# Four graph layers on 32 graphs: the last graph's softmax sums taken by TensorE, layer 2's weights planned later, new entry delays for graphs 1 to 4

## The chip, the core and the metric

The kernel runs on one NeuronCore of one Trainium2 chip. A core has TensorE (PE in the profile; its weight loads are PEld), VectorE (DVE), ScalarE (ACT), GpSimd (POOL) and SyncE (SP), each with its own instruction queue, and 16 DMA engines that all queues share. The metric is the device time of one execution in microseconds (us), as the median of several runs; lower is better.

## The reference, cut to what matters

The input is 32 graphs of 512 nodes with 256 features, `x` of shape (32, 512, 256) in float32, and one adjacency matrix `adj` (512, 512) that all graphs share. Each graph goes through four layers, and each layer is an attention over the graph followed by a residual and a normalisation:

```
x = layernorm(x + L0(x, adj))   # 8 heads, softmax(q k^T / sqrt(32)), then a feed-forward pair w1, w2
x = layernorm(x + L1(x, adj))   # 1 head, e = leaky_relu(s1[i] + s2[j]), softmax, times h = x W
x = layernorm(x + L2(x, adj))   # e = leaky_relu((x W1)(x W2)^T), softmax, times x W3, relu
x = layernorm(x + L3(x, adj))   # 4 heads, e = leaky_relu(e_src[i] + e_dst[j]), softmax, elu
```

In every softmax the entries without an edge are masked out. The kernel computes the unnormalised weights p = exp(e) * edge, multiplies them with the values, and divides by the row sums of p afterwards. How those row sums are formed in layers 0 and 3 is what the change touches.

## The kernel before

**One graph, one chain.** Everything of a graph stays on the chip: a (512, 256) tile is loaded, goes through the four layers, and is stored. Nodes lie in NC = 4 chunks of 128 partitions, features in KC = 2 halves. Matmuls are in float32.

**An order written by a planner.** `fast_path` doesn't issue instructions as it goes. `plan(engine, ns, run, reads, writes, ...)` records an operation with an assumed duration, and `Plan.place` then walks a model of the five engines and of the DMA: again and again it takes the operation that can start earliest, and among those of one engine the one with the earliest due time (`urgency`), and issues it. So the source fixes a static order for each engine's queue. On the chip each engine takes its queue in that order and waits on semaphores. Due times come from graph number times `PACE` plus a curve `TENTHS` over the graph's own ranks; `START` gives the model's earliest time for the first operation of graphs 0 to 4; at most `WAYS` = 5 graphs are open at once. A slot (`p`: 8 buffers of 1 MB, `t`: 9, `bank`: the 8 PSUM banks, and others) is given out only if the graphs ahead can still be completed, which `safe` reads from a profile of how many slots a graph holds at each rank.

**Preparation.** `prepare` (graph -1 in the planner) loads and transforms the weights: `load` issues a DMA from SP and tells the planner with `lag` how long after the issue the data is there. Edge transposes are line 767, the folding of b1 is line 784, the transposes of layer 2's W1 and W2 line 831, and their product line 842. In `urgency`, preparation comes before any graph on every engine but SP.

**Row sums in layer 0.** For each half g and each chunk m, `exps` makes four score products (line 996) and four exponentials (line 1000), DVE multiplies with the edges (line 1018), and PE adds value products into a bank (line 1025). The row sums run beside that: `add_dma` (line 934) has GpSimd issue a DMA that adds one `p` buffer to another, (1 into 0), (3 into 2), (2 into 0); the two totals are then multiplied with a column of ones, `pick`, in line 1042: eight products, four of them in four different 32-column strips at a time. `rinv0` and `heads_out` (lines 947, 956, 979, 982) follow.

**Row sums in layer 3.** A `p` holds two chunks of two heads. DVE makes it in four scalings (line 1238) and one multiplication (line 1245), PE uses it in line 1254. After the second `p` of a half, two DMAs add it to the first and then fold the halves of the result; line 1269 multiplies the totals with `pick`. Lines 947, 964, 979 and 982 divide, lines 1277 to 1282 finish the elu, lines 907 to 917 normalise, and line 1296 stores.

Of the kernel before, what the change touches and what calls it, by code (L numbers as in the profile page):

```python
# [25 lines left out]

WAYS = 5
PACE = 90.76
START = (0, 0, 60.35, 91.65, 156.14)
LAST = ()  # L30
STAY = 3.96
TENTHS = (0, 30.43, 93, 94.94, 170.51, 206.64, 280.32, 312.71, 390.11, 381.83, 480.02)
@with_exitstack
def general_path(
    ctx: ExitStack,
# [408 lines left out]
class Plan:  # L444
# [62 lines left out]
    def place(self, urgency, ways, stay=0.0, run=True):  # L507


        held_by = {g: self.profile(g) for g in {self.ops[0].graph, self.ops[-1].graph}}  # L510
        engines = {e: 0.0 for e in (PE, DVE, ACT, POOL, SP, DMA)}
        waiting = {e: [] for e in engines}
        free = {k: [(0.0, i) for i in range(n)] for k, n in self.counts.items()}
# [9 lines left out]
        def safe(op, kind, new):  # L523
            spare = len(free[kind]) - len(new)
            if spare < 0:
                return False
            have = spare
            for g in order:
                mine = held.get((g, kind), [])
                have += len(mine)  # L530
                if g == op.graph:
                    have += len(new)
                    mine = mine + new
                r, rows = front[g], held_by.get(g, held_by[self.ops[-1].graph])[kind]
                ahead = sorted(s.first for s in mine if s.first > r)
                for i, stop in enumerate(ahead + [len(rows)]):
                    if stop > r and max(rows[r:stop]) + len(ahead) - i > have:
                        return False
                    r = max(r, stop)
                if g == op.graph:  # L540
                    return True
# [70 lines left out]
def fast_path(  # L612
# [87 lines left out]
    def T(slot):  # L700
        return slot.tile if slot.kind is None else buffers[slot.kind][slot.index]
# [23 lines left out]
    odd = keep("odd", [P, NC])  # L725

    def prepare():
        def load(dst, to, src, lag=3000):
            def run():
                with nc.allow_non_contiguous_dma(reason="columns, once"):  # L730
                    nc.sync.dma_start(to(T(dst[0] if isinstance(dst, tuple) else dst)), src)
            plan(SP, 450, run, [], [dst], lag=lag)
# [268 lines left out]
                T(p)[:, j, :], T(banks[j]), AF.Exp, scale=1.0 / math.sqrt(D0)),  # L1001
                [banks[j]], [(p, j)])

    def layer0(xs):
        xT = transposed(xs)
        qT, kT, v = Slot("t"), Slot("t"), Slot("v")
        for k in range(KC):
            project_t(wqkv, C + k * P, xT, kT, k)
            project_t(wqkv, k * P, xT, qT, k)
        project(xT, wqkv, 2 * C, C, v)  # L1010

        oT, sm, totals = Slot("t"), Slot("bank"), []
        for g in range(KC):
            av, ps = Slot("bank"), []
            for m in range(NC):
                p = Slot("p")
                exps(kT, qT, g, m, p)
                dve(2420, lambda p=p, m=m: nc.vector.tensor_tensor(  # L1018
                    T(p), T(p), T(edge_t)[:, m, :].unsqueeze(1).to_broadcast([P, J, N]), ALU.mult),
                    [p, (edge_t, m)], [p], True)  # L1020

                def run(p=p, m=m, g=g, av=av):
                    for j in range(J):
                        h = g * J + j
                        nc.tensor.matmul(T(av)[j * D0:(j + 1) * D0, :],  # L1025
                                         T(v)[:, m, h * D0:(h + 1) * D0],
                                         T(p)[:, j, :], start=(m == 0), stop=(m == NC - 1))
                plan(PE, 880, run, [(v, m), p], [av], tiling=2)
                ps.append(p)
                if m % 2:  # L1030
                    add_dma(ps[m - 1], p)
                if m == 3:
                    add_dma(ps[0], ps[2])
                total = ps[0]

            totals.append(total)
            evac(oT, lambda t, g=g: t[:, g, :], av, lambda b: b, N, [(oT, g)])

        def run():
            for g, p in enumerate(totals):  # L1040
                for j in range(J):
                    nc.tensor.matmul(T(sm)[j * 32:(j + 1) * 32, :], pick[:, g, :], T(p)[:, j, :],  # L1042
                                     start=(g == 0), stop=(g == KC - 1))
        plan(PE, 1740, run, totals, [sm], tiling=2)
        rinv = rinv0(sm)
        t = heads_out(oT, rinv, H0)

        def check():
            r = T(rinv)[:, :NC * H0]
            nc.vector.scalar_tensor_tensor(fit, r, R_MIN, fit, ALU.is_gt, ALU.min)  # L1050
            nc.vector.scalar_tensor_tensor(fit, r, R_MAX, fit, ALU.is_lt, ALU.min)
        dve(370, check, [rinv], [], True)
        for c0 in range(0, NC, 2):
            add(t, t, xs, c0)
        n1 = Slot("y")
        normalise(t, n1)
        for c0 in range(0, NC, 2):
            add(xs, xs, None, c0, be2_row)
        nT = transposed(n1)
        y = Slot("y")  # L1060
        for c0 in range(0, NC, 2):
            add(y, n1, None, c0, g1_row, ALU.mult)
            add(y, y, None, c0, bb_row)
        hT = Slot("t")
        for d in range(KC):
            bank = Slot("bank")

            def run(bank=bank, d=d):
                for k in range(KC):
                    nc.tensor.matmul(T(bank), T(w1_sb)[:, k, d * P:(d + 1) * P], T(nT)[:, k, :],  # L1070
                                     start=(k == 0), stop=(k == KC - 1))
            plan(PE, 1720, run, [w1_sb, nT], [bank])
            act(690, lambda bank=bank, d=d: nc.scalar.activation(
                T(hT)[:, d, :], T(bank), AF.Relu, bias=T(b1_sb)[:, d:d + 1]), [bank, b1_sb], [(hT, d)])
        f = Slot("y")
        for c0 in range(0, NC, 2):
            bank = Slot("bank")

            def run(bank=bank, c0=c0):
                for j in range(2):  # L1080
                    for k in range(KC):
                        nc.tensor.matmul(T(bank)[:, j * C:(j + 1) * C],  # L1082
                                         T(hT)[:, k, (c0 + j) * P:(c0 + j + 1) * P],
                                         T(w2_sb)[:, k, :], start=(k == 0), stop=(k == KC - 1))
            plan(PE, 1730, run, [w2_sb, hT], [bank])
            dve(680, lambda bank=bank, c0=c0: nc.vector.tensor_tensor(
                T(f)[:, c0:c0 + 2, :], T(bank).rearrange("p (c d) -> p c d", c=2),
                T(y)[:, c0:c0 + 2, :], ALU.add),
                [bank, (y, c0), (y, c0 + 1)], [(f, c0), (f, c0 + 1)])
        normalise(f, f)  # L1090
        for c0 in range(0, NC, 2):
            w, parts = slice(c0, c0 + 2), (c0, c0 + 1)
            dve(690, lambda w=w: nc.vector.tensor_tensor(
                T(f)[:, w, :], T(f)[:, w, :], T(g2_row).unsqueeze(1).to_broadcast([P, 2, C]),
                ALU.mult), [(f, c) for c in parts] + [g2_row], [(f, c) for c in parts], True)
            dve(690, lambda w=w: nc.vector.tensor_tensor(
                T(f)[:, w, :], T(f)[:, w, :], T(xs)[:, w, :], ALU.add),
                [(s, c) for s in (f, xs) for c in parts], [(f, c) for c in parts], True)
        return f
# [122 lines left out]
            add(y, y, xs, c0)  # L1222
        return y

    def layer3(xs):
        xT = transposed(xs)
        totals = []
        q, G, oT, sm = Slot("v"), Slot("p"), Slot("t"), Slot("bank")
        project(xT, l3w, 0, C + 2 * H3, q)
        e1, e02 = gates(q, H3, G)  # L1230
        for k in range(KC):
            av = Slot("bank")
            for m0 in range(0, NC, 2):
# [22 lines left out]
                                             T(p)[:, 2 * m + i, :], start=(m0 + m == 0),  # L1256
                                             stop=(m0 + m == NC - 1))
                plan(PE, 1770, run, [q, p], [av], tiling=3)
                if m0 == 0:
                    total = p  # L1260
                else:
                    add_dma(total, p)
                    add_dma(total, None)

            totals.append(total)
            evac(oT, lambda t, k=k: t[:, k, :], av, lambda b: b, N, [(oT, k)])
        def run():
            for h in range(H3):
                nc.tensor.matmul(T(sm)[32 * h:32 * h + 32, :], pick[:, 0, :],  # L1269
                                 T(totals[h // 2])[:, h % 2, :], start=True, stop=True)  # L1270
        plan(PE, 870, run, totals, [sm], tiling=2)
        t = heads_out(oT, rinv3(sm), H3)

        e, y = Slot("y"), Slot("y")
# [10 lines left out]
        return y  # L1285

    def graph(b):
        xs = Slot("x")
        plan(SP, 450, lambda xs=xs: nc.sync.dma_start(
            T(xs), x[b].rearrange("(c p) d -> p c d", p=P)), [], [(xs, c) for c in range(NC)],  # L1290
            lag=9000)
        for layer in (layer0, layer1, layer2, layer3):
            y = layer(xs)
            xs = Slot("x")
            normalise(y, xs)
        plan(SP, 450, lambda: nc.sync.dma_start(
# [80 lines left out]
```

## Time and profile before

| | before |
|---|---|
| median of 3 runs | 3004.08 us (3002.78 to 3010.93) |
| profiled span | 3009.1 us, mean granted TensorE clock 0.985 |
| PE busy | 2903.1 us (96%) |
| DVE, ACT, POOL busy | 2361.4 us (78%), 1963.8 us (65%), 951.3 us (32%) |
| accumulating DMAs of 1 MB, line 934 | 256, 7.6 us median from issue to landing |
| accumulating DMAs of 0.5 MB, line 934 | 64, 5.3 us median |

The page is read from the top: which engine is busy, then in which slices of the span it isn't, then the chain of work that ended last. An engine that is busy in nearly the whole span bounds the kernel in its middle; what is left are the two ends, where the chain of waits names what the engine stood still for.

### The profile page before, as it was taken

The page shows a single profiled execution, that of the slowest core. Times are in us where ns is not written, and L with a number is a line of the kernel's source. Part 1 is how long each engine was busy: PE and PEld are TensorE (multiplying, and loading weights), DVE is VectorE, ACT ScalarE, POOL GpSimd, SP SyncE. Part 2 cuts the span into 40 slices and gives each one's busy share as a digit, 9 for nine tenths or more (in the row PEclk, how much of TensorE's full clock was granted, in tenths as well). Part 3 has the DMA queues.
Part 4 walks back from the last instruction along what each step waited for, and adds up shares of the span by engine and source line. Part 5 has one row for each costly group of instructions (what it writes and reads, how often), then busy time and mean ns, then how long its engine had stood idle before and what let it go on. Part 6 is the DMA issues. An engine that isn't in the chain of part 4 may idle for free.

```text
span 3009.1 us, 40990 instructions
## 1 busy us (share of the span) xinstructions
PE 2903.1 (96%) x14698; PEld 1649.3 (55%) x14698; DVE 2361.4 (78%) x4138; ACT 1963.8 (65%) x4359; POOL 951.3 (32%) x875
## 2 busy tenths in 40 slices
PE   7989999999999999999999999999999999999983
PEld 3455555555555555555555555555555555555551
DVE  4467778888888888887888888888788888888773
ACT  3566766666766666776666776666776666676552
POOL 0222343323333322333322333332233332333211
PEclk9999999999999999999999999999999999999996
DMA  5644755666655566565566566566566566665434
GB/s 142 130 90 97 154 121 118 137 144 133 140 131 116 128 147 140 129 136 118 127 148 137 123 140 132 116 142 137 127 142 132 118 135 144 135 139 125 90 83 97
DMA packets 95155, 385.20 MB, mean 128 GB/s; under 512 B 8928, under 2 KB 44896, under 8 KB 58080
## 3 DMA queue, kind: packets, MB, share of 16 engines
q0 software_dynamic: 46080, 302.01, 51.2%
q1 hardware_dynamic: 48864, 80.49, 7.9%
q8 instruction: 118, 1.93, 0.3%
q14 instruction: 93, 0.76, 0.1%
HBM read 63.38 MB, written 17.10 MB: 27 GB/s over the span
## 4 chain that ended last, share of the span: by engine, by line
PE 91%; DMA 3%; DVE 3%; ACT 1%; issue 1%; POOL 0%; SPq 0%; DVEq 0%; ACTq 0%
PE bank L893 15%; PE bank L879 11%; PE bank L996 9%; PE bank L1025 8%; PE bank L1155 8%; PE bank L1214 7%; PE bank L1254 7%; PE bank L1180 7%; PE bank L866 5%; PE bank L1082 4%; PE bank L1070 4%; PE bank L1042 2%; PE bank L979 2%; PE bank L1203 2%; PE bank L947 1%; PE bank L1269 1%
## 5 line engine op out<-in xcount | busy, mean ns | idle before, releaser
L934 POOL DMA_DIRECT2D p<-p x320 | 289.3, 906 | 1304.0 <-issue 352.9
L1018 DVE TENSOR_TENSOR p<-p,edge_t 128x2048 f32<-128x2048 f32 x256 | 602.3, 2354 | 82.9 <-ACT p L1000 82.9
L1000 ACT ACTIVATE p<-bank 128x512 f32<-128x512 f32 x1024 | 560.1, 597 | 138.5 <-PE bank L996 138.3
L854 ACT ACTIVATE t<-bank 128x512 f32<-128x512 f32 x640 | 372.5, 594 | 364.9 <-PE bank L1254 146.7
L924 POOL TENSOR_TENSOR y<-y,x 128x512 f32<-128x512 f32 x192 | 339.0, 1771 | 358.7 <-ACT y L1219 174.1
L907 DVE BATCH_NORM_STATS2 st<-y 128x6 f32<-128x256 f32 x768 | 315.1, 410 | 66.6 <-POOL y L924 59.0
L996 PE MATMUL bank<-t,t 32*128 32x512 f32 x2048 | 296.3, 645 | 0.0
L1245 DVE TENSOR_TENSOR p<-p,edge_t 128x2048 f32<-128x2048 f32 x128 | 292.8, 2287 | 3.3
L917 ACT ACTIVATE x<-y,rs,rs 128x256 f32<-128x256 f32 x512 | 284.0, 596 | 8.4 <-DVE rs L914 8.1
L1238 DVE TENSOR_SCALAR p<-p,e,e 128x512 f32<-128x512 f32 x512 | 249.6, 540 | 43.3 <-DMA p<-row 37.3
L1025 PE MATMUL bank<-p,v 128*32 128x512 f32 x2048 | 270.1, 610 | 10.6 <-DVE p L1018 10.4
L1155 PE MATMUL bank<-v,p 128*128 128x257 f32 x1024 | 247.9, 387 | 9.3 <-DVE rs L914 7.0
L1254 PE MATMUL bank<-p,v 128*64 128x512 f32 x1024 | 238.5, 607 | 11.7 <-DVE p L1245 11.7
L854 ACT ACTIVATE v<-bank 128x512 f32<-128x512 f32 (+2 forms) x384 | 171.8, 455 | 112.8 <-PE bank L893 109.5
L1180 PE MATMUL bank<-t,t 128*128 128x512 f32 x512 | 238.7, 599 | 0.0
L879 PE MATMUL bank<-t,wqkv 128*128 128x512 f32 x512 | 232.4, 603 | 0.0
L1214 PE MATMUL bank<-v,p 128*128 128x256 f32 x1024 | 230.2, 382 | 0.0
L1155 PEld LDWEIGHTS bank<-v,p 128*128 128x128 f32 x1024 | 188.9, 192 | 70.6 <-issue 26.5
L1214 PEld LDWEIGHTS bank<-v,p 128*128 128x128 f32 x1024 | 191.9, 190 | 48.4 <-ACT t L854 20.5
L917 ACT ACTIVATE y<-y,rs,rs 128x256 f32<-128x256 f32 x256 | 138.9, 595 | 60.4 <-DVE rs L914 60.4
L996 PEld LDWEIGHTS bank<-t,t 32*128 32x128 f32 x2048 | 82.5, 184 | 167.4 <-issue 76.6
L866 PEld LDWEIGHTS bank<-ident,x 128*128 128x128 f32 x1024 | 117.8, 143 | 101.0 <-issue 59.3
(116 smaller groups left out, 4479.6 us busy)
## 6 DMA issues: line engine op xcount, KB each, us to landing
p<-p POOLq DMA_DIRECT2D x256, 1024.0 KB, 7.6
p<-row SPq DMA_DIRECT2D x32, 1024.0 KB, 9.4
p<-p POOLq DMA_DIRECT2D x64, 512.0 KB, 5.3
x<-in_x_dram SPq DMA_DIRECT2D x32, 512.0 KB, 4.0
out_dram<-x SPq DMA_DIRECT2D x32, 512.0 KB, 4.8
e<-row SPq DMA_DIRECT2D x32, 256.0 KB, 6.5
t<-in_adj_dram SPq DMA_DIRECT2D x4, 256.0 KB, 6.5
wqkv<-in_L_gnn_w_qkv_dram SPq DMA_DIRECT2D x1, 768.0 KB
```

Source lines behind the costliest of these rows:

```text
L854: act(170 + n * 0.84, lambda: nc.scalar.activation(to(T(dst)), frm(T(src)), AF.Copy), [src], writes)
L879: nc.tensor.matmul(T(bank), T(w)[:, i, col:col + P], T(xT)[:, i, :], start=(i == 0), stop=(i == KC - 1))
L893: nc.tensor.matmul(T(bank)[:, j * width:(j + 1) * width], T(xT)[:, k, (c0 + j) * P:(c0 + j + 1) * P], T(w)[:, k, col:col + width], start=( ...
L917: act(600, lambda c=c: nc.scalar.activation(T(dst)[:, c, :], T(y)[:, c, :], AF.Identity, bias=T(nm)[:, c:c + 1], scale=T(rs)[:, c:c + 1]), ...
L996: nc.tensor.matmul(T(banks[j]), T(kT)[r, g, m * P:(m + 1) * P], T(qT)[r, g, :], start=True, stop=True)
L1000: act(600, lambda j=j: nc.scalar.activation(T(p)[:, j, :], T(banks[j]), AF.Exp, scale=1.0 / math.sqrt(D0)), [banks[j]], [(p, j)])
L1018: dve(2420, lambda p=p, m=m: nc.vector.tensor_tensor(T(p), T(p), T(edge_t)[:, m, :].unsqueeze(1).to_broadcast([P, J, N]), ALU.mult), [p, ( ...
L1025: nc.tensor.matmul(T(av)[j * D0:(j + 1) * D0, :], T(v)[:, m, h * D0:(h + 1) * D0], T(p)[:, j, :], start=(m == 0), stop=(m == NC - 1))
L1155: nc.tensor.matmul(T(bank)[:, :C + 1], T(p)[:, m, c * P:(c + 1) * P], T(v)[:, m, 2:C + 3], start=(m == 0), stop=(m == NC - 1))
L1180: nc.tensor.matmul(T(bank), T(qT)[:, k, c * P:(c + 1) * P], T(xT)[:, k, :], start=(k == 0), stop=(k == KC - 1))
L1214: nc.tensor.matmul(T(bank)[:, j * C:(j + 1) * C], T(pT)[:, m, c * P:(c + 1) * P], T(v)[:, m, :C], start=(m == 0), stop=(m == NC - 1))
L1254: nc.tensor.matmul(T(av)[i * D3:(i + 1) * D3, :], T(q)[:, m0 + m, 2 * H3 + h * D3:2 * H3 + (h + 1) * D3], T(p)[:, 2 * m + i, :], start=(m0 ...
```

## The change

There are three edits and some bookkeeping.

1. In the last graph (`at_once`), the row sums of layers 0 and 3 are no longer formed by accumulating DMAs. PE multiplies every `p` with `pick` directly and accumulates in the bank `sm`. `skip` puts empty operations in the place of those left out, so that ranks and due times stay aligned with the other graphs. The purpose is that the last graph doesn't wait for DMAs, with nothing behind it to fill the time.
2. The default `lag` of `load` goes from 3000 to 15000 ns. It holds for the weights and vectors of layers 1, 2 and 3, which are loaded last. The planner now takes them to land later and orders the preparation that needs them (lines 814, 831, 842) behind the first work of graph 0.
3. `START` for graphs 1 to 4 is changed, and the last two values of `TENTHS` by 0.4.

`place` now holds a slot profile for each graph, because the last graph's differs.

```diff
-START = (0, 0, 60.35, 91.65, 156.14)
+START = (0, 17.91, 74.63, 79.1, 135.8)
-TENTHS = (0, 30.43, 93, 94.94, 170.51, 206.64, 280.32, 312.71, 390.11, 381.83, 480.02)
+TENTHS = (0, 30.43, 93, 94.94, 170.51, 206.64, 280.32, 312.71, 390.11, 382.2, 480.41)
...
-        held_by = {g: self.profile(g) for g in {self.ops[0].graph, self.ops[-1].graph}}
+        held_by = {g: self.profile(g) for g in {op.graph for op in self.ops}}
...
-        def load(dst, to, src, lag=3000):
+        def load(dst, to, src, lag=15000):
...
+    def skip(n):
+        for _ in range(n):
+            plan(DMA, 0, None)
...
+        def sums(g, p, start, stop):
+            for j in range(J):
+                nc.tensor.matmul(T(sm)[j * 32:(j + 1) * 32, :], pick[:, g, :], T(p)[:, j, :],
+                                 start=start, stop=stop)
+        def collect(g, m, ps):
+            if at_once:
+                for c in (m - 1, m):
+                    plan(PE, 870, lambda c=c: sums(g, ps[c], g == 0 and c == 0,
+                                                   g == KC - 1 and c == NC - 1),
+                         [ps[c]], [sm], tiling=2)
+                skip(m - 1)
+            else:
+                add_dma(ps[m - 1], ps[m])
+                if m == 3:
+                    add_dma(ps[0], ps[2])
...
-        plan(PE, 1740, run, totals, [sm], tiling=2)
+        if at_once:
+            skip(1)
+        else:
+            plan(PE, 1740, lambda: [sums(g, p, g == 0, g == KC - 1) for g, p in enumerate(totals)],
+                 totals, [sm], tiling=2)
...
+        def sums(h, p, part, start, stop):
+            nc.tensor.matmul(T(sm)[32 * h:32 * h + 32, :], pick[:, 0, :], T(p)[:, part, :],
+                             start=start, stop=stop)
...
-                if m0 == 0:
+                if at_once:
+                    plan(PE, 1740, lambda p=p, k=k, m0=m0: [sums(
+                        2 * k + i, p, 2 * m + i, m0 + m == 0, m0 + m == NC - 1)
+                        for m in range(2) for i in range(2)], [p], [sm], tiling=2)
+                    skip(2 if m0 else 0)
+                elif m0 == 0:
                     total = p
                 else:
                     add_dma(total, p)
                     add_dma(total, None)
...
     def graph(b):
+        at_once = b == B - 1
...
-            y = layer(xs)
+            y = layer(xs, at_once) if layer in (layer0, layer3) else layer(xs)
```

More of the change, by code (lines that the diff above doesn't have):

```diff
@@ L533, in safe @@
                     mine = mine + new
-                r, rows = front[g], held_by.get(g, held_by[self.ops[-1].graph])[kind]
+                r, rows = front[g], held_by[g][kind]
                 ahead = sorted(s.first for s in mine if s.first > r)
@@ L1002, in exps, with layer0 @@
                 [banks[j]], [(p, j)])
-    def layer0(xs):
+    def skip(n):
+        for _ in range(n):
+            plan(DMA, 0, None)
+    def layer0(xs, at_once):
         xT = transposed(xs)
@@ L1030, in layer0 @@
                 if m % 2:
[L1031 to L1036, printed above, removed]
-            evac(oT, lambda t, g=g: t[:, g, :], av, lambda b: b, N, [(oT, g)])
[L1039 to L1043, printed above, removed]
-        plan(PE, 1740, run, totals, [sm], tiling=2)
+                    collect(g, m, ps)
+            evac(oT, lambda t, g=g: t[:, g, :], av, lambda b: b, N, [(oT, g)])
+            totals.append(ps[0])
+        if at_once:
[3 more added lines that the diff above has]
+                 totals, [sm], tiling=2)
         rinv = rinv0(sm)
@@ L1223, in layer2, with layer3 @@
         return y
-    def layer3(xs):
+    def layer3(xs, at_once):
         xT = transposed(xs)
@@ L1263, in layer3 @@
                     add_dma(total, None)
-            totals.append(total)
+                    totals.append(total)
             evac(oT, lambda t, k=k: t[:, k, :], av, lambda b: b, N, [(oT, k)])
[L1267 to L1271, printed above, removed]
+        if at_once:
+            skip(1)
+        else:
+            plan(PE, 870, lambda: [sums(h, totals[h // 2], h % 2, True, True) for h in range(H3)],
+                 totals, [sm], tiling=2)
         t = heads_out(oT, rinv3(sm), H3)
```

## The prediction

> **What bounds the kernel now.** I read the slices of the page first, then the table of stages, the waits of PE, and the chain of waits at both ends.
>
> ```profile
> PE   7989999999999999999999999999999999999983
> ...
> PEclk9999999999999999999999999999999999999996
> ```
>
> PE is at 90% or more in 36 of 40 slices. Of the span of 3009.1 us it is idle for 106.0 (3009.1 - 2903.1). The table of stages places that: 17.1 us in the first 20; 19.1 us from 40 to 180; 6.2 us from 200 to 2750, where nearly every stretch of 50 us reads 50.00; 0.7 us from 2750 to 2800; 62.9 us after. In the middle only less PE work would make it faster; at the ends, fewer waits.
>
> ```profile
> 2650.00:2700.00 50.00, 50.00 (x260) 28.69 (x254) 39.37 (x72) 40.44 (x91) 15.27 (x15) 1.00 0.65 145
> ...
> 2800.00:2850.00 50.00, 43.50 (x196) 27.87 (x189) 32.97 (x83) 24.48 (x57) 19.87 (x19) 0.93 0.38 85
> 2850.00:2900.00 50.00, 47.34 (x212) 31.17 (x211) 37.27 (x75) 29.71 (x72) 9.38 (x12) 0.97 0.41 92
> 2900.00:2950.00 50.00, 39.01 (x159) 24.02 (x157) 30.58 (x60) 22.08 (x52) 7.68 (x9) 0.90 0.42 103
> 2950.00:3000.00 50.00, 16.17 (x52) 5.71 (x52) 27.52 (x49) 9.62 (x21) 8.43 (x8) 0.64 0.35 74
> ```
>
> The columns are stretch, length, busy time of PE, PEld, DVE, ACT and POOL, granted clock, DMA share and GB/s. The drain begins at 2800, and in the last 50 us PE has 16 us of work. The waits of PE in the first 60 us:
>
> ```profile
> PE bank L831 <- DMA y<-in_L_gnn_W_dram: 9.0, 1, 9.0
> PE bank L866 <- DMA x<-in_x_dram: 8.1, 1, 8.1
> ```
>
> After graph 0's transposes (8.06 to 10.00) PE stands still until 19.02 for layer 2's W1, though the edges for line 767 were ready at 10.75 (the end of line 759 on DVE). The chain of waits of the tail (start, length, what):
>
> ```profile
> 2962.28 3.70 PE bank L1254 x8
> 2965.99 0.29 issue
> 2966.28 0.51 POOL p L934
> ...
> 2969.33 9.07 DMA p<-p
> 2978.39 0.28 issue
> 2978.68 6.48 DMA p<-p
> 2985.16 0.14 issue
> 2985.30 2.06 PE bank L1269 x8
> 2987.38 0.61 ACT e L854
> ```
>
> The last graph (31) has its last masked p at 2966.38, but its row sums reach PE 19 us later, through two accumulating DMAs in series. From 2987.38 to the end are 21.7 us of division, elu, normalisation and store, which nothing in the change touches.
>
> **What the skill says.** "TensorE: Matmul & The Clock Gate", Architectural detail, has PE's matmuls in program order and ACT and DVE strictly first in, first out. The trace agrees: line 767 lay behind line 831 for 8 us with its operand ready, and DVE stood 14.10 us at line 964 (2933 to 2947), with graph 31's scalings behind it. The same page's part on the HAM clock gate says that an idle window of about 3.4 us halves the clock. The trace shows the direction: after its waits PE has a granted clock of 0.65 from 2950 to 2960, and line 1254's four products take 3.46 us at 2954 and 2.6 us after, against 1.94 at full clock. "TensorEngine Tiling (Array Packing)", Key Properties, says that a change of tiling mode drains the array; layer 3's sums (32 columns) alternate with line 1254 (64 columns). The trace shows no gap at such changes, so I put them at 0, at most 0.1 us each by the planner's own figure, eight of them.
>
> **Part 1, the weights' order.** A lag of 15 us puts lines 831 and 842 behind graph 0's first work. Nothing is removed: their 1.5 + 0.5 + 1.7 us of PE move. Line 767 can then start at 10.75 in place of 20.57, line 784 behind it needs w1, landed at 11.03, and the first projection (879) needs wqkv, issued first of all; its landing isn't shown, but line 879 didn't wait for it. The wait of 9.02 shrinks to 0.75: **-8.3 us**. Between 0 and 9: from 40 to 180 PE waits for graph 0's exponentials (waits for line 1018, 9.9 us in all), and an earlier graph 0 may only wait elsewhere. I keep the whole, because the moved 3.7 us and graph 1 fill such gaps. The scores of line 814 (3.7 us on DVE) move to after 24 us; DVE was idle 7.28 us ahead of its first line 1018, and that hides them or costs up to 3.7.
>
> **Part 2a, layer 0 of graph 31.** Line 1042 does two buffers' sums in 1.85 us of the chain, 0.93 each. Eight buffers take 7.4, so PE does **+5.6 us** more, and it lies before 2782, where PE reads 50.00 of 50: all on the path. Six DMAs (four pairs, two joins) and their POOL issues of 0.87 us go; none bounded the stage. In exchange the last value product (line 1025) ends at 2782.2 and line 1042 starts at 2799.65: graph 31 may go on up to 17.5 us earlier. That doesn't shorten PE's work, only its idle time in the drain, 15.9 us from 2800 to 2934. I take a third, **-5.3 us**; the bounds are 0 (due times hold it back) and 15.9. The sums' bank is held through layer 0 now, one of eight, in one graph: 0.
>
> **Part 2b, layer 3 of graph 31.** After 2966.38 come line 1254 for the last p and its four sums. No row shows sums in two column strips. The lower bound is 0.88, line 1269's four strips at full clock; the upper is line 1254's own form, two strips, 2.6 at the clock found there. I take 2.6, for the clock stays low between DVE's deliveries every 4.15 us. The sums end at 2966.4 + 2.6 + 2.6 = 2971.6 in place of 2987.36: 15.8 less. Bounds: 2969.1 (1.87 + 0.88, full clock) and 2975.2 (PE bound by 4 x 5.3 from 2954), so 18.3 and 12.2. Against it: graph 30's elu adds sat on POOL behind graph 31's line 934 until 2966.9, and its line 1282 and statistics on DVE (2968.5 to 2973.0, 4.5 us) lay in the shadow of the DMAs. Without that wait they are ready near 2954, are due earlier, and go between graph 31's p's. I charge all 4.5: **-11.3 us**. Graph 30's own DMAs stay. The 6 us of extra products lie in PE's idle time.
>
> **Part 3, delays and due times.** Graphs 3 and 4 enter the planner's order 12.6 and 20.3 us earlier, graphs 1 and 2 later by 17.9 and 14.3. The delays hold back nothing on the chip; they reorder. The ramp's largest wait is 7.0 us (161 to 168, PE for DVE's line 1148 and statistics), with nothing from later graphs to do. Earlier graphs 3 and 4 speak for a gain of up to 7, a new order for a loss of up to 5; I take **-2 us**. `TENTHS` and the slot profiles: 0, since the middle is PE-bound in any order that keeps it fed.
>
> Sum: -8.3 + 5.6 - 5.3 - 11.3 - 2 = -21.3, from 3004.1: **2983 us**.
>
> **The rivals.**
> - *The start's gain is given back.* Graph 0 is earlier, but the ramp waits for its exponentials and for DMAs (DMA share 0.97 and 1.03 from 70 to 80 and 90 to 100). Of 8.3 us 3 stay, and the new delays cost 2 in place of giving 2: 2983 + 5.3 + 4 = 2992. For it: PE had only 17.3 and 16.3 busy in the two stretches of 20 us from 60 to 100. Against it: projections fill most of that time.
> - *The drain closes up.* Graph 31, 17.5 us ahead, fills all 15.9 us, and graph 30's end doesn't hinder it (15.8): 3004.1 - 8.3 + 5.6 - 15.9 - 15.8 - 2 = 2968.
> - *The middle loses its fit.* One row sum repeats every 89.28 us (line 1042: 2531.78, 2621.06, 2710.34), with PE full. If the new entry times lock the graphs into a pattern in which PE misses 1.2 us a period, 27 periods cost 32: 2983 + 32 = 3015, slower than before. For it: the order is greedy, and its model of the DMA (5.6 + 2.5 us) isn't the chip's. Against it: DVE at 80% and ACT at 66% leave room, and before, with other delays, the pattern became full by itself after 200 us.
>
> **How the numbers follow.** The main forecast has 0.55, the first rival 0.20, the second 0.17, the third 0.08. The range reaches from 2968, the second rival, to 2997, the first with 5 us for the unknown of line 814 and the sums' form; the third lies outside with the outer edges of the others. Faster means below 2995.1: all of the main case and of the second rival, and most of the first: 0.87. Within 0.3%: 0.08, the upper part of the first and the mild part of the third. Slower: 0.05.
>
> **What would show it.** In the profile after, the PE wait at line 831 is gone and line 767 starts near 11 us; stretches from 200 to 2750 still read 50.00; line 1269 of graph 31 has no DMA ahead of it, its last sum ends 5 to 9 us after the last line 1245, and some 21.7 us follow. Wrong would be: a wait of the size of 9 us in a new place before 200 us, a middle under 50.00, or graph 31's last p later than 2966 minus the start's gain, with graph 30's DVE work ahead of it.

## The result, and the profile after

| | before | changed |
|---|---|---|
| median of 4 runs | 3005.73 us (3002.78 to 3010.93) | 2986.06 us (2984.06 to 2988.57) |
| ratio, 95% interval | | 0.9933 [0.9916, 0.9950] |
| profiled span, mean granted clock | 3009.1 us, 0.985 | 2983.3 us, 0.990 |
| PE busy | 2903.1 us | 2901.5 us |

The changed kernel is 19.7 us faster by the medians, against 21.1 us predicted; the time predicted was 2983, the time measured 2986. The total came out well. Its terms didn't, as the experiments show: the start gives more than was priced, and the drain, which was to give 5.3, gives nothing. That these errors cancelled was luck.

The changed kernel's code has new lines, so its line numbers differ: 1018 (edge multiplication of layer 0) is now 1042, 1025 (its value products) 1049, 1042 (its sums) 1021, 1148 and 1155 (weights and products of layer 1) 1168 and 1175, 1238 and 1245 (scalings and masking of layer 3) 1262 and 1269, 1254 (its products) 1278, 1269 (its sums) 1253, and 1282 (elu) 1310.

First the busy slices from the page of the changed kernel, one digit for each 40th of the span:

```profile
PE   7899999999999999999999999999999999999895
...
PEclk9999999999999999999999999999999999999998
```

The dip of the ramp lies one slice earlier than before (the second, not the third), and the last two slices read 9 and 5 where they read 8 and 3; the slice ahead of them has an 8. The table of stages shows the drain (stretch, length, busy time of PE, PEld, DVE, ACT and POOL, granted clock, DMA share, GB/s):

```profile
2650.00:2700.00 50.00, 50.00 (x239) 26.11 (x232) 42.68 (x76) 35.68 (x84) 6.73 (x11) 1.00 0.69 153
...
2800.00:2850.00 50.00, 41.86 (x177) 27.65 (x173) 35.06 (x86) 29.64 (x69) 13.51 (x14) 0.93 0.30 74
2850.00:2900.00 50.00, 46.81 (x214) 31.77 (x213) 38.01 (x79) 27.44 (x68) 13.20 (x12) 1.00 0.39 90
2900.00:2950.00 50.00, 32.25 (x134) 19.44 (x134) 30.77 (x53) 18.08 (x42) 9.21 (x10) 0.84 0.40 95
2950.00:3000.00 50.00, 14.14 (x74) 4.25 (x70) 20.10 (x41) 8.97 (x19) 2.49 (x2) 0.85 0.07 23
```

The middle is as full as before: PE has 2493.84 us of work from 200 to 2700, against 2493.79. The drain hasn't closed up: from 2800 to 2900 PE works 88.7 of 100 us, before 90.8. The gain lies at the two ends.

At the start, the waits of PE in the first 40 us (what waited for what; us in total, times, longest), and three lines of its timeline there (start, length):

```profile
PE bank L866 <- DMA x<-in_x_dram: 7.9, 1, 7.9
PE bank L1049 <- DVE p L1042: 0.8, 1, 0.8
```

```profile
9.59 3.40 PE L767 MATMUL bank<-ident,p 128*128 128x128 f32 x16
...
24.05 1.04 PE L831 MATMUL bank<-ident,y 128*128 128x128 f32 x8
25.01 1.14 PE L996 MATMUL bank<-t,t 32*128 32x512 f32 x8
```

The wait of line 831 is gone. Graph 0's first scores (line 996) start at 25.01; before they started at 39.26. So graph 0 has won 14.3 us here, and not 8.

At the end, the chain of waits (start, length, what):

```profile
2919.40 10.41 DMA p<-p
2929.81 0.29 issue
2930.10 5.78 DMA p<-p
...
2936.02 1.19 PE bank L1253 x8
...
2941.43 3.90 DVE p L1262 x4
2945.34 2.29 DVE p L1269
...
2957.81 2.30 DVE p L1269
...
2960.15 1.94 PE bank L1278 x8
2962.09 3.61 PE bank L1253 x24
2965.72 0.60 ACT e L854
```

Graph 31's sums end 5.6 us after its last masked p, where before 21.0 us lay between (2966.38 to 2987.36); line 1253, the sums, follows line 1278 with no DMA ahead of it. The two DMAs in the chain are now graph 30's: DVE reaches graph 31's first scalings only after graph 30's sums, which still go that way. And these first four scalings take 3.90 us, where each later group takes 1.9.

Marks in the two profiles, before and after, place the gain:

| mark | before | after | difference |
|---|---|---|---|
| graph 0's layer 0 sums | 102.14 | 85.71 | -16.4 |
| graph 30's layer 0 sums | 2710.34 | 2697.60 | -12.7 |
| graph 31's first scalings in layer 3 | 2949.69 | 2941.43 | -8.3 |
| its last masked p ends | 2966.38 | 2960.10 | -6.3 |
| its sums end | 2987.36 | 2965.70 | -21.7 |
| end of the span | 3009.1 | 2983.3 | -25.8 |

For the rows of sums at layer 0 and of scalings, the time is that of the start. These are single executions: the one profiled before was the slowest of its four (3010.93), and the medians differ by 19.7, not 25.8. The last step (4 us between the sums' end and the end of the span) is taken up below.

### The profile page after: what moved, and what is told of

The parts are those of the page before. It is cut to its first block, busy times and chain, and to the rows that moved or that the text cites. A ratio compares the mean times of both kernels' runs of the same rounds, so it can differ in the third digit from the quotient of the medians.

```text
span 2983.3 us, 41104 instructions
## 1 busy us (share of the span) xinstructions
PE 2901.5 (97%) x14770; PEld 1645.9 (55%) x14770; DVE 2371.4 (79%) x4138; ACT 1962.9 (66%) x4359; POOL 946.7 (32%) x865
## 4 chain that ended last, share of the span: by engine, by line
PE 93%; DVE 3%; DMA 2%; ACT 1%; issue 0%; POOL 0%; SPq 0%; ACTq 0%; DVEq 0%
PE bank L893 15%; PE bank L879 11%; PE bank L996 9%; PE bank L1049 8%; PE bank L1175 8%; PE bank L1234 7%; PE bank L1278 7%; PE bank L1200 7%; PE bank L866 5%; PE bank L1102 4%; PE bank L1090 4%; PE bank L1021 2%; PE bank L1223 2%; PE bank L979 2%; PE bank L1253 1%; PE bank L947 1%
## 5 line engine op out<-in xcount | busy, mean ns | idle before, releaser
L934 POOL DMA_DIRECT2D p<-p x310 | 280.7, 908 | 1228.5 <-issue 290.2
L854 ACT ACTIVATE v<-bank 128x258 f32<-128x258 f32 (+2 forms) x384 | 171.8, 455 | 111.7 <-PE bank L893 108.5
L1234 PEld LDWEIGHTS bank<-v,p 128*128 128x128 f32 x1024 | 191.6, 190 | 49.1 <-ACT t L854 20.5
## 6 DMA issues: line engine op xcount, KB each, us to landing
e<-row SPq DMA_DIRECT2D x32, 256.0 KB, 6.7
t<-in_adj_dram SPq DMA_DIRECT2D x4, 256.0 KB, 6.3
```

The costliest lines, as they stand in the source:

```text
L854: act(170 + n * 0.84, lambda: nc.scalar.activation(to(T(dst)), frm(T(src)), AF.Copy), [src], writes)
L1234: nc.tensor.matmul(T(bank)[:, j * C:(j + 1) * C], T(pT)[:, m, c * P:(c + 1) * P], T(v)[:, m, :C], start=(m == 0), stop=(m == NC - 1))
```

## The experiments

Apart from the edit shown, each kernel is the changed kernel's code with parts of the change switched off, so the line numbers are those of the changed kernel. Each was timed in five rounds beside the kernel before; "before" in the table is its median in the same set of runs.

| run | median us | before | difference | ratio [95%] |
|---|---|---|---|---|
| e1_lag_only | 2994.09 | 3010.78 | -16.7 | 0.9943 [0.9930, 0.9957] |
| e2_start_only | 3107.29 | 3010.78 | +96.5 | 1.0318 [1.0304, 1.0332] |
| e3_layer3_only | 2993.45 | 3010.78 | -17.3 | 0.9945 [0.9931, 0.9958] |
| e4_layer0_only | 3019.91 | 3010.78 | +9.1 | 1.0031 [1.0022, 1.0040] |
| e5_start_but_graph4 | 3008.85 | 3010.35 | -1.5 | 0.9994 [0.9986, 1.0002] |
| e6_after_again | 2989.72 | 3010.35 | -20.6 | 0.9935 [0.9922, 0.9949] |
| e7_after_old_start | 2992.84 | 3010.35 | -17.5 | 0.9945 [0.9932, 0.9959] |
| e8_after_layer0_by_dma | 2984.25 | 3010.35 | -26.1 | 0.9914 [0.9901, 0.9928] |
| e9_lag_layer3 | 2982.22 | 3010.24 | -28.0 | 0.9910 [0.9895, 0.9925] |
| e10_before_own_tiles | 3007.91 | 3010.24 | -2.3 | 0.9995 [0.9986, 1.0003] |
| e11_lag_layer3_own | 2980.14 | 3010.24 | -30.1 | 0.9897 [0.9881, 0.9913] |
| e12_lag_two_graphs_own | 2977.71 | 3010.24 | -32.5 | 0.9890 [0.9874, 0.9905] |

**e1: the weights' order alone.** The kernel before, with one number changed.

```diff
-        def load(dst, to, src, lag=3000):
+        def load(dst, to, src, lag=15000):
```

> The kernel before with one edit: the default lag of the weight loads 15000 in place of 3000. Theory A (each part acts at its own place, the parts add): PE's wait of 9 us at line 831 goes and nothing takes its place, so graph 30's layer 0 sum (before: 2710.3) comes 8 us earlier, and the time falls by 8 us, 6 to 10. Rival B (the order as a whole decides): the ramp gives the gain back, graph 30's sum moves by less than 4 us, and the time falls by 0 to 4.

Measured: 16.7 us faster, twice the 8.3 priced and outside of both theories. The timeline of PE in this kernel shows the same head as the changed kernel:

```profile
24.73 1.04 PE L831 MATMUL bank<-ident,y 128*128 128x128 f32 x8
25.69 1.14 PE L996 MATMUL bank<-t,t 32*128 32x512 f32 x8
```

and of the kernel before:

```profile
19.02 1.54 PE L831 MATMUL bank<-ident,y 128*128 128x128 f32 x6 [9.02 <-DMA y<-in_L_gnn_W_dram]
...
28.83 1.89 PE L842 MATMUL bank<-t,t 128*128 128x256 f32 x8
...
39.26 2.00 PE L996 MATMUL bank<-t,t 32*128 32x512 f32 x16
```

The first scores come 13.6 us earlier. 9.0 of it is the wait. About 3.1 is work ahead of them that has moved behind (line 831's 1.54 + 0.67 and line 842's 1.89, less the 1.04 of line 831 that stays). The rest, 1.5 us, is the same work in less time: line 784's eight products take 0.95 in place of 1.71, line 879's sixteen take 7.11 in place of 3.20 + 5.31 (a later x takes a little of that back). The sums of layer 0 then start earlier by 17.3 us in graph 0 (102.14 to 84.80), 21.2 in graph 1 (150.37 to 129.16), 17.0 in graph 2 (223.99 to 207.04) and 14.1 in graph 30 (2710.34 to 2696.22). The moved work now runs where PE would wait: line 842 comes at 27.26, between graph 0's first and second scores, and the first masked p still lets PE wait 1.63 us at 32.44. In the first 180 us PE idles 25.0 us, before 36.1, so 11 us of idle time are gone where the wait was 9.

One profile of each kernel can differ by some us. All of them together say the same: graph 30's layer 0 sums start between 2706.6 and 2712.4 in the five profiles with the old order of weights (before, e3, e4, e5, e10; e2 left out), and between 2693.5 and 2697.2 in the five with the new order and the old delays (e1, e7, e9, e11, e12). The means differ by 13.8 us, which is what the first scores have won.

**e2: the new delays alone.**

```diff
-START = (0, 0, 60.35, 91.65, 156.14)
+START = (0, 17.91, 74.63, 79.1, 135.8)
-TENTHS = (..., 390.11, 381.83, 480.02)
+TENTHS = (..., 390.11, 382.2, 480.41)
```

> The kernel before with one edit: the new START and TENTHS. Theory A: the delays matter little by themselves; of the 12.7 us by which graph 30's layer 0 sum came earlier after the change, 8.3 are the lag's, so here 4 us less, 0 to 6. Rival B: the new delays carry most of the gain of the ramp, 8 to 12 us less. Rival C: without the lag they don't fit, 0 to 8 us slower.

Measured: 96.5 us slower, far outside of what any theory allowed for this part. The table of stages of this kernel:

```profile
40.00:180.00 140.00, 124.68 (x656) 56.45 (x652) 79.37 (x96) 81.71 (x168) 38.61 (x35) 0.96 0.62 126
180.00:250.00 70.00, 46.69 (x168) 29.51 (x167) 26.81 (x62) 26.69 (x60) 3.14 (x4) 0.88 0.04 15
250.00:300.00 50.00, 26.46 (x101) 14.84 (x102) 20.09 (x35) 10.74 (x25) 6.65 (x9) 0.76 0.34 69
```

and the middle of these rows in the kernel before:

```profile
180.00:250.00 70.00, 70.00 (x365) 40.66 (x364) 46.41 (x96) 47.22 (x107) 20.98 (x18) 1.00 0.32 66
```

No engine is near full from 180 to 300: PE idles 46.9 of 120 us. Score products of graph 2's layer 0 (line 996) stop at about 156 and resume at 311.42; its sums come at 341.80, before at 223.99. One graph was held up while the others ran dry. In the planner's own placement for this `START`, which doesn't depend on the chip, graph 2 gets four `bank` slots for its scores at 141.4 us of planned time and then not before 299.4: its guard `safe` refuses them until 298.0, while the first transposes and projections of graph 4 were let in at 145 to 164. That points to graph 4's earlier entry (135.8 in place of 156.14), which e5 tests. The planner's total holds the whole loss too: its last operation starts at 3060.8 us here and at 2963.9 for the kernel before, 96.9 later. So this loss could have been read off before any run. The plan isn't a forecast in general, though: for e1 it ends 0.7 us later than for the kernel before.

**e3: layer 3 of the last graph alone**, by TensorE; layer 0 and all else as before.

```diff
-        at_once = b == B - 1
+        at_once = {layer0: False, layer3: b == B - 1}
...
-            y = layer(xs, at_once) if layer in (layer0, layer3) else layer(xs)
+            y = layer(xs, at_once[layer]) if layer in (layer0, layer3) else layer(xs)
```

> The kernel before with one edit: the last graph's layer 3 sums by direct products (layer 0's by DMA as before). Theory A: everything until the last graph's scalings stays, and the end of the sums comes 15 us earlier: the time falls by 15 us, 11 to 18. Rival B: graph 30's elu and statistics move between the last graph's buffers and a new wait on DVE takes half: 7 to 10 us less.

Measured: 17.3 us faster, where 11.3 were priced. Its chain of waits ends so:

```profile
2960.32 7.07 PE bank L1278 x24
2967.38 3.61 PE bank L1253 x24
2971.01 0.60 ACT e L854
```

The last masked p ends at 2964.41, its sums at 2970.99: 6.6 us where 21.0 were. That alone is 14.4 us. Graph 30's elu (line 1310) and statistics start on DVE at 2964.33, right with the end of the last masking, in the time in which PE does products and sums. The 4.5 us charged for their going in between weren't paid. But graph 31's first four scalings take 3.81 us, before 1.90, so 1.9 of the gain are lost there, and what is left is 12.5. The rest of the 17.3 isn't in this part: its interval reaches from 13 to 21 us, and this execution was 3.7 us ahead of the one before at graph 30's layer 0 sums already (2706.61), where nothing had been changed yet.

**e4: layer 0 of the last graph alone.**

```diff
+        at_once = {layer0: b == B - 1, layer3: False}
```

> The kernel before with one edit: the last graph's layer 0 sums by direct products (layer 3's by DMA as before). Theory A: eight times 0.97 us less 1.9 us of PE work more in a stretch where PE is full, and 1 us of it won back in the drain: 4 us slower, 2 to 6. Rival B: the last graph runs ahead by the 17 us of its DMA chain and the drain closes up: 5 to 10 us faster.

Measured: 9.1 us slower. In the profiles PE is busy 2910.0 us in place of 2903.1 (+6.9, against 5.6 priced for the products), and idle 112.9 in place of 106.0. How the 9.1 divide isn't settled by that: the profiled execution took 3024.64, 4.7 above this kernel's median, and busy times of kernels with the same products differ by up to 5 us (2898.3 in e10). The waits of PE from 2700 on show a new wait; this kernel, and then the kernel before:

```profile
PE bank L1175 <- DVE p L1168: 11.1, 2, 7.3
```

```profile
PE bank L1155 <- DVE p L1148: 2.3, 2, 1.9
```

It is the same wait, of layer 1's products for the weights that DVE makes, and it has grown from 2.3 to 11.1 us. It goes with layer 0's part in every profile: 7.3 to 11.1 us in the four that have it (e4, e6, e7, the changed kernel), 2.2 to 3.9 in the others; its longest piece is 7.3 us in all four, 1.9 or 2.8 in the others. That the masking is slow (line 1168 takes 5.3 us there) isn't the reason: in seven of the others it takes 5.15 us, under a wait of 1.9. As I read it, graph 31 enters layer 1 earlier, relative to graph 30, and the products that had covered this wait are done by then. From graph 30's layer 0 sums to graph 31's last masked p it takes 270.7 us, before 256.0; 262.5 to 270.7 in the four, 254.6 to 260.7 in the others.

**e5: the new delays without graph 4's.** As e2, with one value of the old kept.

```diff
-START = (0, 17.91, 74.63, 79.1, 135.8)
+START = (0, 17.91, 74.63, 79.1, 156.14)
```

> As the run with the new START and TENTHS alone (which took 96 us more than before), but graph 4 keeps its old delay of 156.14. Theory A (graph 4, let in 20 us earlier, takes buffers while graph 2 is still in layer 0, and the planner then refuses graph 2 the banks for its next scores): the hole of 180 to 300 us goes and the time is that of the kernel before, within 8 us. Rival B (graphs 2 and 3, let in 4.5 us apart, are the cause): still 80 us or more slower.

Measured: no difference from before that can be told.

```profile
180.00:250.00 70.00, 70.00 (x357) 40.44 (x356) 46.92 (x97) 48.59 (x109) 20.58 (x17) 1.00 0.30 61
```

PE is busy for 70.00 of the 70 us from 180 to 250, and graph 2's sums come at 222.11. Graph 4's entry is the cause of the hole in e2; the other three delays, with the new `TENTHS`, are worth nothing on their own that shows.

**e6: the changed kernel again**, without an edit, for comparison on the same chip.

> The changed kernel itself, on the same chip as the others of this call, as their yardstick: ratio to the kernel before 0.993, 19 to 25 us less.

**e7: the changed kernel with the old delays.**

```diff
-START = (0, 17.91, 74.63, 79.1, 135.8)
+START = (0, 0, 60.35, 91.65, 156.14)
```

(`TENTHS` as before, too.)

> The changed kernel with the old START and TENTHS. Theory A (with the lag the new delays gain little): 2 to 6 us above the changed kernel. Rival B (the new delays were needed to make use of the lag): 8 us or more above it. Rival C: nothing, within 2 us.

Measured: 3.1 us slower than e6, with intervals that overlap. The delays that cost 96 us by themselves cost nothing once the weights are out of graph 0's way. They don't speed up the ramp: graph 2's sums come at 205.84 in e7 and at 209.88 in e6.

**e8: the changed kernel with layer 0's sums by DMA.**

```diff
+        at_once = {layer0: False, layer3: b == B - 1}
```

> The changed kernel with the last graph's layer 0 sums by DMA again (layer 3's direct). Theory A (the direct sums of layer 0 cost 5 to 9 us of PE and the drain gives nearly nothing back, as the run with layer 0 alone showed with 9 us slower): 3 to 9 us below the changed kernel. Rival B (with layer 3 direct, the last graph's head start pays): 2 to 6 us above it.

Measured: 5.5 us faster than e6, with intervals that overlap. PE's wait for line 1168 in the drain is 3.9 us (in the slowest of its five executions), in e6 and the changed kernel 8.4. So layer 0's part seems to cost in the whole change too; e9 against e7, below, shows it clear of noise.

**e9: the weights' order and layer 3, nothing else.** Old delays, layer 0 by DMA.

> The kernel before with two edits: the lag of 15000 and layer 3's direct sums in the last graph; old START and TENTHS, layer 0's sums by DMA. Theory A (the parts act at the two ends and add): 16.7 + 17.3 = 34 us below the kernel before, 30 to 37. Rival B (the new delays with both are as good or better): no more than 26 us below, as the changed kernel with layer 0 by DMA was.

Measured: 28.0 us faster. The two parts alone sum to 34.0, but each of the three ratios has an interval of some 4 us to either side, so the 6 us between aren't resolved. By the profiles nothing is lost: 13.8 us of the start and 12.5 of layer 3 make 26.3.

A price that layer 3's part has is the first group of graph 31's scalings; in e9, and then in e1:

```profile
2935.53 3.88 DVE L1262 TENSOR_SCALAR p<-p,e,e 128x512 f32<-128x512 f32 x4
```

```profile
2934.10 1.92 DVE L1262 TENSOR_SCALAR p<-p,e,e 128x512 f32<-128x512 f32 x4 [0.48 <-DMA p<-row]
```

It takes 2.0 us longer. In e9 POOL does graph 30's elu adds (line 924) from 2936.00 to 2938.67, beside it; in e1 they come at 2951.30, after the last masking, since on POOL they lie behind line 934, which waits to issue graph 31's DMA. e3 pays the same, so its 17.3 contains it.

With e6 to e8 there is now a table of four, all with the new order of weights and layer 3 by TensorE:

| | layer 0 by DMA | layer 0 by TensorE | cost of layer 0's part |
|---|---|---|---|
| old delays | e9, -28.0 | e7, -17.5 | 10.5 |
| new delays | e8, -26.1 | e6, -20.6 | 5.5 |

Of e7 and e9 the intervals lie apart, of e6 and e8 they don't. And layer 0's part comes with an advantage that isn't its own: in e6 and e7 the final check ends early, in e8 and e9 it doesn't. What that is worth, e10 and the end of the next section tell.

**e10: the final check with tiles of its own**, in the kernel before. The last instructions of the kernel reduce the running extremes `fit`, `far` and `odd` to one flag, in small tiles that they share with the normalisations.

```diff
-    bad, col, total = buffers["rs"][:3]
+    bad, col, total = (const.tile([P, NC], FP, name=n) for n in ("bad", "col", "total"))
```

> The kernel before, but the final check of the flag has three tiles of its own in place of three buffers of the kind rs. Theory A (in the kernel before, the check's two reductions wait until the last normalisation has left those buffers, and the flag, not the last store, ends the program; the changed kernel's new order happened to free them earlier, which gave 4 us): 3 to 5 us below the kernel before, and the reductions stand earlier in the profile. Rival B (the last store ends it in any case): no change, within 1 us.

Measured: -2.3 us, and not resolved. The profile shows what the edit does: the reductions on DVE no longer follow the last normalisation. The last store is issued at 3000.94 and the span ends 5.4 us later; before, the flag came at 3000.53, the store at 3000.66, and the end 8.4 us after the store. In the profile the step from the sums' end to the end of the span is 3.0 us shorter (18.7, before 21.7), with the same PE times in it.

**e11 and e12: towards a better version.** e11 is e9 with e10's edit; e12 also takes layer 3 of the last two graphs to TensorE.

```diff
-        at_once = {layer0: False, layer3: b == B - 1}
+        at_once = {layer0: False, layer3: b >= B - 2}
```

> Lag, layer 3's direct sums and the check's own tiles, old START. Theory A: 4 us below the run without own tiles, 38 below the kernel before. Rival B: as that run, within 1 us.

> As the last one, but the last two graphs take layer 3's sums directly. Theory A: graph 30's sums (16 us of DMA in the chain) no longer hold DVE's queue, but graph 31's scalings wait for their broadcast, which lands about when those sums do, and 6 us of PE work are added beside waits: 0 to 3 us below the one-graph version. Rival B: the chain of DMAs was what graph 31 waited for: 5 to 12 us below it.

Measured: -30.1 and -32.5. Each step gives about 2 us, of the size of the intervals. In e12 DVE passes graph 30's line 964 at 2924.50, in e11 at 2934.28; yet graph 31's last masked p ends only 2.5 us earlier (2952.8 and 2955.3), since other work takes the place of the wait: graph 31's own scalings start at 2936.13, in e11 at 2936.60. e12 is the fastest version here. It is 12 us faster than e6, the changed kernel, each taken against the kernel before it ran beside (0.9890 and 0.9935, intervals apart).

## Why the prediction came out right, and where its steps failed

**Part 1, the weights' order: right cause, too small.** The step that failed is "The wait of 9.02 shrinks to 0.75: -8.3 us", with its bound "between 0 and 9", and the sentence that "Nothing is removed: their 1.5 + 0.5 + 1.7 us of PE move". That counts PE's time. But PE has idle time in the ramp, and the first graph's chain goes through PE's queue: whatever stands ahead of graph 0 there, be it a wait or work, delays the chain by its length, and work moved into idle time costs nothing. The chain is 13.6 us shorter at the first scores, and the run alone gave 16.7, with an interval from 13 to 21. The Trainium skill's page "TensorE: Matmul & The Clock Gate", Step-by-step: what each phase is for, has PE's matmuls stay in program order; the trace agrees, with line 767 starting at 20.36 behind line 831, and at 10.02 in e1 with line 831 behind it. I had cited this page and still counted only the wait, not the work in the same queue. The 0.75 was a misreading besides: 10.75 is the end of line 795, and the last of line 759 ends at 10.41; e1 shows no wait there at all.

**Part 2a, layer 0: the cost right, the gain not there.** The prediction had +5.6 for PE and "I take a third, -5.3 us" for the drain. The second is the step that failed. Alone the part costs 9.1 us, with the rest of the change 5.5 to 10.5; even 6.9 us for the products, as in e4's profile, would leave nothing won in the drain, and the stretch from graph 30's layer 0 sums to graph 31's last masked p is longer in all four profiles with this part. What I had left out is that a head start isn't free: PE's work stays the same, so what graph 31 does earlier is missing later as cover. By the trace it is missing at line 1168.

**Part 2b, layer 3: right, charged too much.** Of "-15.8 less 4.5", the 15.8 was measured as 15.4 (21.0 to 5.6 us between the last masked p and the sums) in the changed kernel, and 14.4 in e3. The price of 2.6 us for a group of four sums fits the one that went alone (1.95 in the changed kernel, 2.54 in e3), but three groups go together behind the last product, in 3.61 us, so the two errors nearly cancel. The step that failed is "go between graph 31's p's. I charge all 4.5": graph 30's DVE work ran after the last masked p, at 2960.02 to 2963.4 in the changed kernel. The reading that its adds on POOL would come earlier was right, and that had another price: they ran beside graph 31's first scalings, which took 2 us longer (1.9 in e3). So the charge was 2, not 4.5, and the part gave some 12.5 in place of 11.3.

**Part 3, the delays: the sum right, the reason not.** I took -2, and e6 against e7 gives -3.1, which isn't resolved. My reason was that the ramp has idle time for earlier graphs 3 and 4; the ramp got no faster by them. My bound of 5 us for a loss was far off: without the other edits the same delays cost 96.5 us, through graph 4's entry and the guard `safe` (e2, e5). The third rival, that the middle loses its fit, named the danger and sized it at 32 us; it was real, but it is one hole, not a beat that repeats, and the new order of weights removes it.

**The end: not foreseen.** The prediction has "some 21.7 us follow" after the sums, "which nothing in the change touches". In the changed kernel's profile 17.6 us follow. Line 1357, the first reduction of the check, comes at 2903.52 and the flag (line 1365) at 2969.32, before the last normalisation, so the store ends the program and not the flag. Of the four us about one is PE's: lines 947 and 979 took 1.11 and 1.91 us here before, and take 0.66 and 1.04 in the changed kernel and in e3, where the flag still comes last and 20.5 follow. The other three belong to the flag. Which buffers the planner hands to the check decides it: all four kernels with layer 0's part have the early flag, and of the others only those with tiles of their own. In timed runs e10 and e11 put its worth at about 2 us, unresolved in both.

**Why the total fitted.** Added up from the timed runs, -16.7 - 17.3 + 9.1 - 3.1 (the last from e7 and e6) makes -28.0, against -20.6 for the whole in e6. The intervals are too wide to make a loss of that. With the gains that the profiles show for the two ends, 13.8 at the start and 14.4 less 1.9 in layer 3, the sum is -20.3. Against the prediction's terms that is 5.5 more at the start, 1.2 more in layer 3 and 1.1 more from the delays, and 8.8 less in layer 0. So the right total rests on two errors that cancelled, and that was luck.

Of the prediction's own signs, the lost wait, the full middle and the sums 5 to 9 us after the last masking came true. One for failure came half true: graph 31's last p was to come no later than 2966 minus the start's gain, which is 2958, and it came at 2960.1, though graph 30's DVE work didn't lie ahead of it. With the start's real gain of 12.7 it would have been due at 2953.7. Of the 6.4 us, 2.0 are the slow first scalings and 4.4 lie ahead of them, in the drain where the wait for line 1168 has grown.

**What stays open.** How layer 0's 9.1 us divide between its products and the drain. That the wait for line 1168 grew because its cover was used up is read from the trace, not tested: no run moved that cover back. In the start, no run parts the wait from the moved work, nor PE's lines from the other preparation that the lag moves (line 814 on DVE). And the gains of e11 over e9 and of e12 over e11 are each too small for their intervals.

## What to carry to other kernels

At the start of a pipelined kernel, price an edit by the first graph's chain: count the waits and also the work that stands ahead of it in its engine's queue, for PE's idle time there is no measure of the gain. Latency that was hidden on DMAs is worth taking back only where nothing is left to hide it, in the last stage of the last graph; one stage earlier, on a full engine, it costs its products and, as the trace reads here, the cover of a later wait as well. And the entry delays of a planned order aren't knobs of their own: the same four numbers cost 96 us with one order of weights, and nothing with another. Ask the plan first: its own end time showed that loss, if not the gain at the start.

## What the runs showed of the hardware

**DVE can slow down beside POOL, and the order of starts matters.** Four scalings of 128x512 take 1.9 us alone and 3.88 beside two adds on POOL; the line of POOL that ran beside them in the changed kernel, which has 3.88 there too, is this:

```profile
2941.90 2.67 POOL L924 TENSOR_TENSOR y<-y,x 128x512 f32<-128x512 f32 x2 [8.26 <-ACT y L1307]
```

The scalings lose 2.0 of 2.67. In the seven profiles in which the adds lie there they take 3.81 to 3.89, in the others 1.90 to 1.92. A masking of layer 1 (line 1168, 128x2048 with two inputs) takes 2.26 to 2.29 us alone and 5.31 here, where POOL adds from 2801.64 to 2805.63, 3.15 us of it beside:

```profile
2802.48 5.31 DVE L1168 TENSOR_TENSOR p<-p,edge_t 128x2048 f32<-128x2048 f32 x1
```

But overlap alone doesn't slow it. In the profile of the kernel before, 94 such multiplications (lines 1018, 1148, 1245) overlap an add of line 924 by more than 0.3 us. The 30 that began while an add was running all took longer, 2.68 us or more and 2.93 at the median. Of the 64 that began before the add, 63 took their usual 2.27 to 2.30; the other began only 0.10 us before it and took 5.15. The Trainium skill's page "SBUF — State Buffer", SBUF: two separate sides, has the two engines share one pair of ports under an exclusive lock when DVE has two inputs in SBUF or runs in a two-port mode; who starts first holds it for the whole instruction, and the other blocks. For the multiplications the trace agrees, with these counts. It matters where DVE is on the path that sets the end, as it was for graph 31.

**A flag at the end costs more than a store.** The flag decides a branch of the program, whose other side doesn't run. Where it is formed last, the span ends 8.2 to 8.6 us after it, in all seven profiles of that kind; before, and in the changed kernel, its last instruction is

```profile
3000.53 0.14 DVE L1335 TENSOR_SCALAR beyond<-rs 1x1 int32<-1x1 f32 x1
```

```profile
2969.32 0.14 DVE L1365 TENSOR_SCALAR beyond<-rs 1x1 int32<-1x1 f32 x1
```

with the end at 3009.1 and 2983.3. Where it is formed early, as in the changed kernel, the span ends with the last store, 5.1 to 5.6 us after its issue, in all seven profiles of that kind (2978.12 to 2983.3 here, 5.4 in e10). What fills these times the profiles don't show.
